# A two-layer graph convolution: 40 tiles of edges summed from h instead of 32, and denser lists of single rows

## The chip, the core and the metric

The kernel runs on one core of one Trainium2 chip. The metric is the time of one execution on the device, in microseconds (us). Five engines work beside each other, each in its own order: PE (TensorE, with its weight loads as PEld), DVE (VectorE), ACT (ScalarE), POOL (GpSimd) and SP (SyncE). SP, ACT and POOL also issue DMAs.

## The reference

There are N = 12500 nodes with 128 features and E = 200000 edges, sorted by their destination. An edge has a source, a destination and one of R = 8 types. Two layers of a relational graph convolution are followed by a residual and a layer norm:

```
W[r]     = sum_b comp[l, r, b] * basis[l, b]              # 8 matrices of 128 x 128
msg[e]   = h[src[e]] @ W[type[e]]
mean[n,r]= sum of msg over the edges (dst = n, type = r) / max(their number, 1)
h_new[n] = relu(sum_r mean[n, r] + h[n] @ root[l] + bias[l])
h        = h_new + h                                      # after layer 1 and after layer 2
out      = layernorm(x + h)                               # over the 128 features
```

## The kernel before, in words

**Tiles and octets.** The edges are cut into 1563 tiles of 128. Eight tiles are an octet (`Q = 8`); there are 196 octets in a layer, the last of 3 tiles. Each layer is one loop over the octets. A tile's 128 source rows are brought in by one indirect DMA (L814, POOL), and PE multiplies them with a 128-column or 256-column matrix that DVE makes from the destinations (L1240): it has the edge's weight, 1 over its count, where a column stands for the edge's destination, and zeros elsewhere.

**Layer 1** gathers rows of x, sums them by destination and type (L1340), multiplies by the eight W[r] (L1372) and places the result in the nodes' accumulator (L1403). When 128 nodes are done, they become a column tile of `h`, which stays in SBUF with features on the partitions (98 node tiles); and the products of these nodes with all eight W[r] of layer 2 go to a table `y_d` in HBM of 100000 rows, one for each node and type (L1558).

**Layer 2** gathers rows of that table by (source, type) and adds them straight into the nodes' accumulator (`add_rows`, L1726): two PSUM tiles in turn, 256 columns each.

**POOL's queue** holds nothing but gathers. A gather of octet q + 5 is issued at step q (`AHEAD = 5`) into one of seven buffers (`rows_r`), and it waits until PE is through with the octet that had the buffer before. The last gathers (from octet 190 on) also wait for the newest octet that PE was given before them (`after`, the cell `done`).

Two things take tiles off POOL's queue in layer 2:

*Lists of single rows* (`lists[1]`, `lone_rows`). A tile of a list isn't gathered; its 128 rows are brought in by 128 DMAs of one row each, with addresses from registers, in chunks of 32. One list is on SP's queue, one on ACT's, each with four host tiles (`sT_f`) in turn. A list takes the tiles from t0 to t1 in steps of `by`. A chunk stands in its queue's order up to 15 octets ahead of its use, one chunk an octet on ACT. SP's queue also holds the loads of x and the stores of the result, and ACT's the square roots of the norms (L1834).

*Octets summed from h* (`SUMMED`, `summed`). An entry `served: (first, end)` says that octet `served` isn't gathered from the table; its sums of source rows are made from `h` in a pass over all 98 node tiles, spread over the octets first to end. For each node tile PE turns it (L1610, `turn`), DVE copies it out of PSUM (L1618) and makes a one-hot matrix of the octet's 1024 sources (L1619, `ready`), and one octet later PE multiplies the two into two PSUM banks, 512 columns each (L1628, `sums`). In the four octets after a pass DVE and PE turn, weigh and multiply the result by W[r] (L1641 to L1674), and at octet `served` one matmul adds it to the accumulator (`place_sums`, L1698). A pass takes its node tiles evenly: `takes[first + j * n // NT]`, with n its number of octets.

**Order inside a step q of layer 2.** POOL: the gathers of q + 5. SP and ACT: chunks of the lists. DVE: copies and one-hots of the pass (`summing(q, 0)`). PE: `add_rows(q)`. DVE: the matrices of octet q + 2, which wait until PE has read octet q's, in one of two buffers. PE: the pass's matmuls and the turning of its next node tiles (`summing(q, 1)`). Then one step of a norm, if one is under way (`todo`): after eight node tiles are done, 1024 rows are turned back, added to x and normalized; the square root is a step on ACT, and DVE's reciprocal of it (L1838) comes six steps later. At every second octet a node tile is finished (L1424, L1428, L1447).

The order on every engine is thus fixed by the program; an engine waits where a semaphore tells it to, and what stands behind the waiting instruction on the same engine waits too.

Of the kernel before, what the change touches and what calls it, by code (L numbers as in the profile page):

```python
# [428 lines left out]
def ordered_path(  # L429
# [60 lines left out]
    DONE = NT - 4  # L490
    LONG = 9
    JOINED = [(1112, 84, 132), (1504, 135, 183)]
    SUMMED = {52: (3, 45), 98: (49, 91), 144: (95, 137), 190: (141, 183)}
    assert D == P and R * K == P and B == BF + 1 and 1 < TL and LAST < P and BF % 4 == 0 and Q == G and N % 2 == 0
    main = slice(HALO, HALO + P)

# [182 lines left out]
    def floats(t, n):  # L679
        return t[:, n * P:(n + 1) * P]  # L680

    sT_f = [t.rearrange("p r g k -> p (r g k)") for t in sT_r.tiles]
# [6 lines left out]
    def hot_cells(c):  # L689
# [4 lines left out]
                                     (sel.rearrange("p g k -> p (g k)"), ["sel"], [])]),  # L694
         ("ACT", 13 * Q + 2, 46 * Q, 8 * Q, 16, 10, [(floats(yr_f, j), yr_cells, yr_cells) for j in range(5)]),
         ("ACT", 53 * Q + 2, 1552, 8 * Q, 16, 10, [(floats(mixer_f, j), ["mixer"], []) for j in range(2)])],
        [("SP", 62, 1552, 49, 32, 15, [(floats(sT_f[0], j), [("sT", 0, 0), ("sT", 0, 1)], []) for j in range(4)]),
         ("ACT", 63, 1552, 49, 32, 15, [(floats(sT_f[1], j), [("sT", 1, 0), ("sT", 1, 1)], []) for j in range(4)])]]
    single, at_row = [{}, {}], [0, 0]
    for l in range(L):  # L700
        for k, (_, t0, t1, by, _, _, hosts) in enumerate(lists[l]):
# [84 lines left out]
    def gather(l, q):  # L786
        if q >= NQ or l == 1 and q in SUMMED:
            return
# [433 lines left out]
    dms, sT, ys, pl, ym = {}, {}, {}, {}, {}  # L1222
    acc, carry, vs, xs, xT, wide = {}, {}, {}, {}, {}, {}

    def onehot(l, q, g=None):

        if q >= NQ and (g is None or g < 0) or l == 1 and q in SUMMED:
            return
# [453 lines left out]

    sums_of = [(s - 1, *summed(i, s, *SUMMED[s])) for i, s in enumerate(sorted(SUMMED))]

    def summing(q, part):
        for end, *f in sums_of:
            if SUMMED[end + 1][0] - LONG <= q <= end:
                f[part](q)

    def place_sums(q, k, opens, last):  # L1690
        t, c = pl.pop(q)
        o, oc = ys.pop(q)
        a, ac = acc[k]
        root_in = opens and k >= 0
        reads = [c, oc] + ([("h", k), ("w", 1, R)] if root_in else [])

        def emit():
            ins = nc.tensor.matmul(a, o, t, start=opens, stop=last and not root_in)  # L1698
            if root_in:
                ins = nc.tensor.matmul(a[:, :rows_of(k)], w_sb[:, 1, R, :], hT[:, k * P:k * P + rows_of(k)],  # L1700
                                       start=False, stop=last)
            return ins

        pe(emit, reads, [ac])
        plan.mark("PE")

    def add_rows(q, k, opens, last, between_last=None):
        if q in SUMMED:
            place_sums(q, k, opens, last)
# [363 lines left out]
    for q in range(AHEAD):  # L2073
        gather(1, q)
    summing(min(a for a, _ in SUMMED.values()) - LONG, 0)
    for n in range(2):
# [66 lines left out]
def kernel(  # L2143
# [18 lines left out]
    flag = ctx.enter_context(tc.tile_pool(name="flag", bufs=1))  # L2162
    bad = flag.tile([1, 1], I32, name="bad")
    plan = ordered_path(tc, bad, x, src, dst, et, basis, comp, root, bias, out)
    every = [mybir.EngineType.PE, mybir.EngineType.Activation, mybir.EngineType.DVE, mybir.EngineType.Pool,
             mybir.EngineType.SP]
# [36 lines left out]
```

## Time and profile before

| what | us |
|---|---|
| median of 3 runs (lowest, highest) | 3730.01 (3728.68, 3738.03) |
| the profiled execution | 3738.43 |
| its span, first to last instruction | 3736.6 |
| POOL busy / PE busy / DVE busy | 2812.0 / 2986.0 / 2354.0 |
| layer 1's gathers, first to last | 4.5 to 1882.1 |
| layer 2's gathers, first to last | 1882.4 to 3723.9 |

A line of the costliest groups reads: line, engine, operation, out<-in by the program's names, shapes, count; then the group's busy time and the mean ns of one; then the idle time of the engine just before these instructions and what ended it. "issue" as the cause means that the engine waited for nothing that the profile shows. In a list of instructions in order of time the columns are the start, the length, the engine and line, and in brackets the idle time before and what ended it. A matmul of 32-bit floats shows as two records. Matmuls are pipelined, so a length is more than the step from one start to the next.

### The profile page before, as it was taken

The numbers are of one execution on the slowest core, as the hardware profiler recorded it, in microseconds if no ns is written. First come the engines' busy times: TensorE is split into PE (matmuls) and PEld (weight loads), VectorE is DVE, ScalarE is ACT, GpSimd is POOL, SyncE is SP. The second block draws the span as 40 slices with busy tenths as digits, with TensorE's granted clock in tenths as the row PEclk, the third lists the DMA queues.
The fourth block names the chain that finished last, engine by engine and source line by source line (L and its number), as shares of the span: only waits on it lengthen the run. The fifth ranks groups of instructions, "written<-read, shape, count | busy, mean of one in ns | idle before, by whom it ended". The sixth has DMA issues, their size and how long they took to land.

```text
span 3736.6 us, 69352 instructions
## 1 busy us (share of the span) xinstructions
PE 2986.0 (80%) x13831; PEld 2137.2 (57%) x13831; DVE 2354.0 (63%) x5786; ACT 354.5 (9%) x795; POOL 2812.0 (75%) x2977
## 2 busy tenths in 40 slices
PE   5777757778877778877778888888888888798896
PEld 3666645565655556655555555555555555555554
DVE  5556435545554445445456778787777787787885
ACT  1121212111111111111100000000000000000000
POOL 7777777777777777777777777777777777777776
PEclk7999889989999999999989999999999999999998
DMA  4122123334333333332332222222222222222222
GB/s 126 55 62 61 56 89 106 117 115 123 112 101 100 91 104 106 95 106 92 99 97 56 55 56 67 67 62 67 56 73 62 62 67 62 67 66 56 68 66 61
DMA packets 159970, 299.91 MB, mean 80 GB/s; under 512 B 67108, under 2 KB 90358, under 8 KB 159534
## 3 DMA queue, kind: packets, MB, share of 16 engines
q0 software_dynamic: 95008, 194.77, 20.4%
q10 hardware_dynamic: 34755, 68.94, 5.7%
q1 hardware_dynamic: 29771, 31.73, 3.2%
q14 instruction: 325, 2.66, 0.2%
q8 instruction: 111, 1.82, 0.2%
HBM read 236.52 MB, written 58.65 MB: 79 GB/s over the span
## 4 chain that ended last, share of the span: by engine, by line
POOL 47%; issue 17%; PE 16%; DMA 9%; ACTq 4%; ACT 3%; DVE 2%; SPq 1%; POOLq 0%; DVEq 0%
POOL rows L814 47%; DMA rows<-y_d,idy 7%; PE y L1372 4%; ACTq L750 3%; PE s L1340 3%; PE s L1726 2%; PE pt L1558 1%; ACTq L745 1%; PE ct L1531 1%; ACT sT L663 1%; SPq L750 1%; ACT y_row L663 1%; DVE dm L1240 1%; PE ct L1010 1%; PE ct L1011 1%
## 5 line engine op out<-in xcount | busy, mean ns | idle before, releaser
L814 POOL DMA_INDIRECT rows<-in_x_dram,idx x1499 | 1420.0, 947 | 459.8 <-issue 451.1
L814 POOL DMA_INDIRECT rows<-y_d,idy x1469 | 1390.0, 946 | 449.8 <-issue 440.2
L1726 PE MATMUL s<-dm,rows 128*128 128x256 f32 x2932 | 777.2, 417 | 260.7 <-DMA rows<-y_d,idy 235.8
L1240 DVE TENSOR_SCALAR dm<-cols,near,w 128x256 f32<-128x256 f16 x1531 | 709.6, 537 | 386.1 <-PE s L1726 376.4
L1726 PEld LDWEIGHTS s<-dm,rows 128*128 128x128 f32 x2932 | 592.4, 210 | 376.4 <-DMA rows<-y_d,idy 233.7
L1240 DVE TENSOR_SCALAR dm<-cols,kr,w 128x128 f32<-128x128 f16 x1563 | 525.9, 403 | 137.4 <-PE s L1340 112.5
L1372 PE MATMUL y<-w_sb,sT 128*128 128x128 f32 x3136 | 443.8, 300 | 203.9 <-ACT ys L663 150.6
L1372 PEld LDWEIGHTS y<-w_sb,sT 128*128 128x128 f32 x3136 | 406.7, 209 | 240.3 <-ACT ys L663 177.6
L1340 PEld LDWEIGHTS s<-dm,rows 128*128 128x128 f32 x2998 | 382.2, 201 | 184.0 <-issue 159.1
L1340 PE MATMUL s<-dm,rows 128*128 128x128 f32 x2998 | 401.6, 287 | 100.5 <-DMA rows<-in_x_dram,idx 90.4
L1619 DVE TENSOR_TENSOR arena<-arena,cols 128x1024 f32<-128x1024 int32 x264 | 319.9, 1212 | 0.0
L1628 PE MATMUL pt<-arena,idx 128*128 128x512 f32 x528 | 269.6, 592 | 0.0
L1628 PE MATMUL y<-arena,idx 128*128 128x512 f32 x528 | 269.6, 592 | 0.0
L1558 PE MATMUL pt<-w_sb,arena 128*128 128x512 f32 (+1 forms) x386 | 206.3, 616 | 63.0 <-DVE y_row L666 43.9
L666 DVE COPY y_row<-pt 128x512 f32<-128x512 f32 x56 | 38.7, 692 | 309.9 <-PE pt L1558 309.9
L663 ACT ACTIVATE sT<-s 128x512 f32<-128x512 f32 x391 | 213.4, 605 | 87.0 <-PE s L1340 86.7
L1516 DVE TENSOR_TENSOR arena<-arena,cols 128x512 f32<-128x512 f32 (+1 forms) x196 | 125.7, 683 | 115.0 <-PE ct L1531 112.2
L1531 PE MATMUL ct<-arena 128*128 128x512 f32 x392 | 187.1, 600 | 0.0
L663 ACT ACTIVATE y_row<-pt 128x512 f32<-128x512 f32 (+1 forms) x139 | 83.0, 597 | 1044.1 <-PE s L1340 846.8
L1628 PEld LDWEIGHTS y<-arena,idx 128*128 128x128 f32 x528 | 100.3, 190 | 126.3 <-issue 126.3
L1619 DVE TENSOR_TENSOR y_row<-arena,cols 128x1024 f32<-128x1024 int32 x128 | 155.1, 1212 | 0.0
L1834 ACT ACTIVATE st<-st,eps 128x8 f32<-128x8 f32 x12 | 3.7, 310 | 1543.8 <-DMA sT<-y_d 1302.3
(253 smaller groups left out, 2300.0 us busy)
## 6 DMA issues: line engine op xcount, KB each, us to landing
sT<-y_d SPq DMA_DIRECT2D x3968, 0.5 KB
sT<-y_d ACTq DMA_DIRECT2D x3968, 0.5 KB
y_d<-y_row ACTq DMA_DIRECT2D x96, 512.0 KB
mixer<-in_x_dram ACTq DMA_DIRECT2D x2304, 0.5 KB
rows<-in_x_dram,idx POOLq DMA_INDIRECT x1499
rows<-y_d,idy POOLq DMA_INDIRECT x1469
jmp<-in_x_dram SPq DMA_DIRECT2D x1408, 0.5 KB
comp_sb<-in_x_dram SPq DMA_DIRECT2D x1408, 0.5 KB
```

Of the source, the lines that this page charges most:

```text
L663: act(lambda: nc.scalar.activation(out_t, in_t, AF.Copy), reads, writes)
L750: return [eng.dma_start(o[j * ch + i:j * ch + i + 1, :].bitcast(byte), table_b[bass.ds(v, 4 * D)].rearrange("(p d) -> p d", p=1)) for i, v ...
L814: ins.append(nc.gpsimd.indirect_dma_start(out=t[:, i - q * Q, :], out_offset=None, in_=table_t, in_offset=bass.IndirectOffsetOnAxis(ap=ids ...
L1240: emits.append(lambda i=i: nc.vector.tensor_scalar(t[:, i - q * Q, :wide], cols[:, :wide], ids[:, i:i + 1], w[:, i:i + 1], op0=ALU.is_equa ...
L1340: last = nc.tensor.matmul(s_b[i // 4][0][:, i % 4, :], lones[i][0] if i in lones else t[:, i, :], d[:, i, :], start=True, stop=True)
L1372: last = nc.tensor.matmul(y[:m], t[:, r, :nt, :].rearrange("p t k -> p (t k)"), w_sb[:, 0, r, :], start=(r == 0), stop=(r == R - 1))
L1516: vec(lambda j=j, p=p, o=o: nc.vector.tensor_tensor(o[:p], e_t[:p], x_node[:p, j:j + 1].to_broadcast([p, M * P]), op=ALU.is_equal), [e_c, ...
L1531: pe(lambda j=j, p=p, i=i, t=t, o=o: nc.tensor.matmul(b.rearrange("p t c -> p (t c)"), t[:p, i * D:(i + 1) * D], o[:p], start=j == 0, stop ...
L1558: pe(lambda: nc.tensor.matmul(hb[:n].rearrange("p r d -> p (r d)"), hT[:, j * P:j * P + n], w_sb[:, 1, k * H:(k + 1) * H, :].rearrange("p ...
L1619: vec(lambda j=j, e=e: nc.vector.tensor_tensor(e, edge, node_p[:, j:j + 1].to_broadcast([P, Q * P]), op=ALU.is_equal), [edge_c, "node"], h ...
L1628: pe(lambda j=j, m=m, o=o, e=e, h=h, b=b: nc.tensor.matmul(b.rearrange("p t c -> p (t c)"), o[:m], e[:m, 4 * h * P:4 * h * P + 4 * P], sta ...
L1726: ins = nc.tensor.matmul(a, lones[i][0] if i in lones else t[:, i, :], d[:, i, :], start=(opens and i == 0), stop=(last and i == n - 1 and ...
```

## The change

Five octets are summed from h in layer 2 instead of four (40 tiles instead of 32). The passes have 34, 34, 34, 34 and 33 octets, where four had 43 each; the gaps of three octets between passes and the end of the last pass at octet 183 are the same. The summed octets are 44, 80, 117, 155 and 191, where they were 52, 98, 144 and 190. The two lists of single rows of layer 2 take every 47th tile instead of every 49th, from the same first tiles: 32 tiles each instead of 31, the last ones 1519 and 1520 instead of 1532 and 1533. Nothing else is edited; layer 1 does the same work.

```diff
-    SUMMED = {52: (3, 45), 98: (49, 91), 144: (95, 137), 190: (141, 183)}
+    SUMMED = {44: (3, 36), 80: (40, 73), 117: (77, 110), 155: (114, 147), 191: (151, 183)}
...
-        [("SP", 62, 1552, 49, 32, 15, [(floats(sT_f[0], j), [("sT", 0, 0), ("sT", 0, 1)], []) for j in range(4)]),
-         ("ACT", 63, 1552, 49, 32, 15, [(floats(sT_f[1], j), [("sT", 1, 0), ("sT", 1, 1)], []) for j in range(4)])]]
+        [("SP", 62, 1552, 47, 32, 15, [(floats(sT_f[0], j), [("sT", 0, 0), ("sT", 0, 1)], []) for j in range(4)]),
+         ("ACT", 63, 1552, 47, 32, 15, [(floats(sT_f[1], j), [("sT", 1, 0), ("sT", 1, 1)], []) for j in range(4)])]]
```

## The prediction

> **What bounds the kernel now.** I read the page first (busy shares, the chain, the costliest groups), then three stretches of the span, then the waits of layer 2, then engines in order of time where the change adds work.
>
> ```profile
> span 3736.6 us, 69352 instructions
> ...
> PE 2986.0 (80%) x13831; PEld 2137.2 (57%) x13831; DVE 2354.0 (63%) x5786; ACT 354.5 (9%) x795; POOL 2812.0 (75%) x2977
> ...
> POOL 47%; issue 17%; PE 16%; DMA 9%; ACTq 4%; ACT 3%; DVE 2%; SPq 1%; POOLq 0%; DVEq 0%
> ...
> L814 POOL DMA_INDIRECT rows<-in_x_dram,idx x1499 | 1420.0, 947 | 459.8 <-issue 451.1
> L814 POOL DMA_INDIRECT rows<-y_d,idy x1469 | 1390.0, 946 | 449.8 <-issue 440.2
> ```
>
> PE has the largest busy share, yet the chain is POOL's. Layer 2's 1469 gathers cost 1390.0 + 449.8 = 1839.8 us, 1.2524 us each, and of the idle part 440.2 us is "issue": POOL waiting for nothing that the profile shows. With layer 1's 1499 gathers (1879.8 us) that is 3719.6 of 3736.6 us. One gather more or less is 1.25 us of the span as long as nothing makes POOL wait.
>
> ```profile
> 400.00:600.00 200.00, 127.08 (x767) 105.04 (x768) 83.83 (x261) 33.56 (x75) 151.43 (x160) 0.86 0.27 84
> 2400.00:2600.00 200.00, 180.01 (x631) 117.12 (x630) 163.90 (x354) 0.31 (x1) 151.33 (x160) 0.97 0.28 64
> 1882.00:3724.00 1842.00, 1562.70 (x5536) 1039.03 (x5535) 1391.63 (x3001) 9.56 (x22) 1390.98 (x1471) 0.94 0.28 65
> ```
>
> ```profile
> POOL rows L814 <- issue: 431.7, 1413, 0.3
> DVE dm L1240 <- PE s L1726: 360.0, 136, 13.0
> PE s L1726 <- DMA rows<-y_d,idy: 237.6, 101, 7.4
> ```
>
> The stretches (PE, weight loads, DVE, ACT, POOL, then the clock) show POOL at the same 151 us in 200 in either layer. In layer 2 PE is busy 85% and DVE 76%, but PE's long wait is for gathered rows and DVE's is for PE: both follow POOL.
>
> **The change, part by part.** *Gathers.* A fifth octet is summed from h instead of gathered: 8 tiles less. The two lists of single rows grow from 31 to 32 tiles each: 2 less. 10 x 1.2524 = 12.5 us off POOL. That is the whole gain, if the rest stays hidden.
>
> *PE and DVE in a pass.* The fifth pass adds 98 node tiles, and a pass has 34 octets for 43, so up to 3 node tiles fall on an octet, 2.9 on the mean for 2.3.
>
> ```profile
> 2411.04 0.49 PE L1610 MATMUL ct<-ident,arena 128*128 128x128 f32 x3
> 2411.37 0.60 PE L1726 MATMUL s<-dm,rows 128*128 128x256 f32 x2
> ...
> 2412.02 3.19 PE L1726 MATMUL s<-dm,rows 128*128 128x256 f32 x14
> 2415.05 1.02 PE L1628 MATMUL pt<-y_row,idx 128*128 128x512 f32 x2
> 2415.91 1.02 PE L1628 MATMUL y<-y_row,idx 128*128 128x512 f32 x2
> ```
>
> ```profile
> 2479.28 3.71 DVE L1240 TENSOR_SCALAR dm<-cols,near,w 128x256 f32<-128x256 f16 x8 [1.56 <-PE s L1726]
> 2482.90 0.20 DVE L1838 RECIPROCAL st<-st 128x8 f32<-128x8 f32 x1
> ...
> 2483.45 0.29 DVE L1618 COPY idx<-ct 128x128 f32<-128x128 f32 x1
> 2483.65 1.22 DVE L1619 TENSOR_TENSOR arena<-arena,cols 128x1024 f32<-128x1024 int32 x1
> 2484.78 0.29 DVE L1618 COPY idx<-ct 128x128 f32<-128x128 f32 x1
> ```
>
> From start to start on PE: seven tiles take 3.03 us, so eight 3.46; half of a node tile's work 0.86, so a node tile 1.72; three transposes 0.33. An octet with three node tiles is 3.46 + 5.16 + 0.33 = 8.95 us at full clock, 9.5 at layer 2's mean clock of 0.94. On DVE eight one-hots take 3.62 and a node tile 1.33: 3.62 + 3.99 = 7.6, some 8.4 with the finish and a share of the norms. POOL's octet after the change is 8 x (1 - 64/1523) = 7.66 gathers, 9.6 us. Both stay under it, PE only just. Over the whole layer PE goes from 1562.7 to about 1562.7 + 98 x 1.72/0.94 + 98 x 0.11/0.94 - 8 x 0.43 = 1750 us, 96% of 1829.5; DVE to 1391.6 + 98 x 1.33 = 1522, 83%. The fifth summed octet's own last steps (24 small matmuls, copies) are some 5 us on PE, and SP gets one more load of an octet's indices; both lie inside the same slack. I cost this at nothing. The cover is POOL's time; if it were gone, the price would be PE's 187 us.
>
> *How far PE may be late.* There are 7 row buffers, so POOL waits for PE only when PE ends an octet later than six octets of gathers, 6 x 9.6 = 57.6 us, after that octet's last gather.
>
> ```profile
> 3603.05 11.00 DMA rows<-y_d,idy
> 3615.01 3.02 PE s L1726 x14
> ```
>
> Here a gather lands 11.0 us after its issue and PE is through 15.0 us after it. Some 42 us stay spare.
>
> *Single rows.* The lists issue 256 more one-row DMAs on SP and ACT, which also issue everything else there in order. ACT carries the norm's square root between them, and DVE's reciprocal waits for it.
>
> ```profile
> 1904.81 265.62 ACTq L750 DMA_DIRECT2D sT<-y_d  x640
> ...
> 2172.82 162.08 ACTq L750 DMA_DIRECT2D sT<-y_d  x384
> 2334.95 0.31 ACT L1834 ACTIVATE st<-st,eps 128x8 f32<-128x8 f32 x1 [162.88 <-DMA sT<-y_d]
> 2337.27 120.27 ACTq L750 DMA_DIRECT2D sT<-y_d  x288
> 2457.59 0.31 ACT L1834 ACTIVATE st<-st,eps 128x8 f32<-128x8 f32 x1 [122.33 <-DMA sT<-y_d]
> ```
>
> ```profile
> 2335.30 0.20 DVE L1838 RECIPROCAL st<-st 128x8 f32<-128x8 f32 x1 [1.49 <-ACT st L1834]
> ```
>
> ```profile
> L1838 DVE RECIPROCAL st<-st x12: 195/198/205, 2185.5 to 3719.3; 128x8 f32<-128x8 f32 x12
> ```
>
> ACT issues without a pause: (2457.59 - 1904.81) / 41 chunks of 32 = 13.5 us a chunk, 54 us a tile. With 195 octets in 1842 us an octet is 9.45 us, so a list needed a tile every 49/8 x 9.45 = 58 us; now every 47/8 x 9.38 = 55 us. ACT still keeps up, but hardly catches up. It starts late (the second root already holds DVE up by 1.49 us), and now stays so. In the changed order of instructions 44 chunks stand ahead of the third root, 41 before: it comes 3 x 13.5 = 40 us later, at 2498, while DVE wants it at 2482.9. So DVE will wait some 15 us there. By the same count for the others (20, 32, 41, 52, 63, 72, 84, 94, 104, 115 chunks become 21, 32, 44, 54, 65, 76, 87, 98, 108, 120), set against the twelve reciprocals' starts less the gathers saved by then, I estimate that seven of the first ten norms wait, 5 to 20 us each, some 70 us in all. DVE is in order: behind its reciprocal stand the copies and one-hots that PE needs. But a single wait of 20 us is less than the 42 spare, norms are some 150 us apart, and PE wins back up to 9.6 - 8.95 = 0.65 us an octet in a pass and about 5 in each of four octets without node tiles, some 40 us per pass. So: nothing, bounded by 0 and 28 us (70 less the 42 spare).
>
> *Tail.* Passes still end at octet 183; the last summed octet is 191, not 190.
>
> ```profile
> 3688.10 0.95 POOL L814 DMA_INDIRECT rows<-y_d,idy  x1 [0.30 <-issue]
> 3690.39 0.95 POOL L814 DMA_INDIRECT rows<-y_d,idy  x1 [1.33 <-PE s L1726]
> ...
> 3722.93 0.95 POOL L814 DMA_INDIRECT rows<-y_d,idy  x1 [0.30 <-issue]
> ```
>
> Octet 192's gathers wait for PE's octet 189, 1.03 us beyond the usual 0.30. With octet 190 gathered between them, 7 gathers rather than 6, that wait may go: 0 to 1 us, I take 0.5. The 12.7 us after the last gather stay.
>
> *Sum.* The profiled execution took 3738.43 us, 3736.6 of span and 1.8 around it. 12.5 + 0.5 = 13.0 off gives 3725.4. The median of the runs shown, 3730.0, is 8.4 under the profiled one, so against it 3717.0, 0.35% less.
>
> *A rule that speaks against it.* The row: POOL's gather takes 947 ns in layer 1 and 946 in layer 2, though DVE's share doubles between the two stretches (83.83 to 163.90 us of 200). The Trainium skill (SBUF — State Buffer, "SBUF: two separate sides") says that VectorE and GpSimd share a port pair that is locked for a whole instruction, so that DMAs issued from GpSimd starve while VectorE runs certain operations. By that rule the added 130 us of DVE would hold POOL for up to that long; by the row it holds it for nothing.
>
> **The rivals.** *The late root reaches POOL (slower).* Place: DVE's reciprocal behind ACT's roots. If PE wins back nothing of what it loses, 70 us less 42 spare = 28 us of POOL waits, 3717 + 28 = 3745. It decides once PE ends an octet over 57.6 us behind its last gather. For it: the second root above comes late even now. Against: the slack per pass.
>
> *PE becomes the pass's bound.* At the clock of the poorest stretch, 0.86, the octet is 8.95/0.86 = 10.4 us, 0.8 x 34 = 27 us lost per pass against 20 to 25 regained between passes; after five passes the spare is used up or nearly so: 0 to 15 us, 3725. For it: PE at 96%. Against: the clock is 0.97 where PE is busiest. The Trainium skill (TensorE: Matmul & The Clock Gate, Part 1) says the clock is halved after idle windows, and the two stretches agree.
>
> *Single rows late at the end.* ACT's last tile is issued 128 x 0.42 = 54 us later and needed 13 us earlier. If ACT slows by a few per cent, PE waits where nothing follows that could hide it: 5 to 15 us, about 3727.
>
> *DVE's lock on POOL.* If POOL is held for a quarter to all of the 130 us, 3750 to 3847.
>
> **How the numbers follow.** The forecast has 0.68. Of that 0.06 falls within 0.3% (11.2 us, about what a measurement of this kernel can tell from no change), because 13.0 is so near it and the runs shown spread over 9 us. The late root has 0.13, PE's bound 0.08 (half of it within 0.3%), late single rows 0.07 (within), the lock 0.02, anything else slower 0.02. So faster 0.62, same 0.06 + 0.04 + 0.07 = 0.17, slower 0.13 + 0.04 + 0.02 + 0.02 = 0.21. The forecast's own range is 3711 to 3721 (12.5 to 13.5 off, with some 4 us of scatter on the median). The range of 8 in 10 reaches on over PE's bound and the late rows, to 3733; the late root and the lock stay outside.
>
> **What would show it.** Layer 2 with 1459 gathers, still 1.25 us each with "issue" as releaser, POOL's wait for PE under some 10 us: the gain is right. PE's wait for rows far below 237.6 us and PE's busy share in a pass above 90%: the ledger is right. Reciprocals of the norms that wait for ACT, 5 to 20 us each: the late root is right, and harmless if POOL does not wait. Wrong if POOL's gathers wait for PE in the middle of passes, if the gather's mean leaves 946 ns, or if over 13 us pass between the last gather and the end.

## The result, and the profile after

The changed kernel takes 3740.79 us (median of 9 runs, 3735.93 to 3742.77), the kernel before 3730.61 beside it: a ratio of 1.0026, with a 95% interval from 1.0018 to 1.0035. So it is 0.26% slower, where 0.35% less was forecast (3717.0 us, range of 8 in 10 from 3711 to 3733). The gathers became fewer as said; the time came back in two waits at the end.

From the page of the changed kernel: span, busy shares, the chain, and the group of layer 2's gathers.

```profile
span 3740.5 us, 71111 instructions
...
PE 3086.4 (83%) x14347; PEld 2170.8 (58%) x14347; DVE 2485.0 (66%) x5990; ACT 354.5 (9%) x795; POOL 2801.9 (75%) x2967
...
POOL 30%; PE 25%; issue 15%; ACTq 12%; SPq 10%; DMA 4%; DVE 3%; ACT 2%; POOLq 0%; DVEq 0%
...
L814 POOL DMA_INDIRECT rows<-y_d,idy x1459 | 1380.1, 946 | 465.2 <-issue 437.2
```

There are 10 gathers fewer, of the same 946 ns. But of 465.2 us of idle time 28.0 are no longer "issue" (before: 9.6), and the chain has moved: POOL from 47% to 30%, SP's and ACT's queues from 5% to 22%. POOL's instructions in order of time show where it waits (start, length, and in brackets the idle time before and what ended it):

```profile
3675.40 0.94 POOL L814 DMA_INDIRECT rows<-y_d,idy  x1 [9.01 <-PE s L1726]
...
3682.90 0.94 POOL L814 DMA_INDIRECT rows<-y_d,idy  x1 [0.30 <-issue]
3694.94 0.94 POOL L814 DMA_INDIRECT rows<-y_d,idy  x1 [11.10 <-PE s L1726]
```

These are the first gathers of octets 190 and 192. The gathers from octet 190 on are issued two octets ahead of PE, not five (`CLOSE = 2`), and wait for PE's newest octet, 187 and 189 here. Before, the only such wait was 1.33 us. The account of the two traces closes to 0.4 us: 12.5 us of gathers less, 19.5 us of waits more there (20.1 less twice the usual 0.30), 1.0 us for the old wait and some 1.1 us at the layer's opening less, together +4.9; the last gather ends at 3728.4 us, where it was 3723.9.

The two traced executions are only 3.9 us apart (3738.43 and 3742.31), the medians 10.2. The rest is probably the pace of the gathers, which is not the same in every execution: from the start of one to the start of the next pass 1251 to 1252 ns in both of these traces, in layer 1 too, but 1249 ns in four traces of the experiments on chips where the kernel before takes 3730 to 3737 us. Over 2960 gathers that is an estimated 7 us, and the traced execution of the kernel before lies 7.8 us above the median. No execution of the kernel before at the faster pace was traced, so this stays open; by it the change costs some 4 us at the same pace, and ratios that lie less than 0.002 apart don't rank two kernels by themselves. The waits in the traces do.

Why PE is late, in three views of the changed kernel. First the waits of layer 2 (total, times, longest):

```profile
PE s L1726 <- DMA rows<-y_d,idy: 58.8, 30, 7.7
DVE arena L1619 <- DMA arena<-in_src_dram: 51.1, 2, 33.9
DVE st L1838 <- ACT st L1834: 47.3, 5, 20.1
```

PE's wait for gathered rows fell from 237.6 us: it follows POOL no longer. DVE waits twice for the indices of a summed octet, loaded by SP, and for roots of ACT. Next SP's DMAs in order of time, each row a group issued one behind the other:

```profile
3329.79 17.54 SPq L750 DMA_DIRECT2D sT<-y_d  x44
3347.39 0.48 SPq L660 DMA_DIRECT2D arena<-in_src_dram  x1
...
3515.25 0.38 SPq L660 DMA_DIRECT2D out_dram<-x_g  x1
3531.09 0.36 SPq L660 DMA_DIRECT2D x_g<-in_x_dram  x1
3533.76 151.67 SPq L750 DMA_DIRECT2D sT<-y_d  x384
```

The indices that DVE waits for until 3364.4 leave SP only at 3347.4, behind chunks of the list. Between the store of a result and the load of x into its buffer SP stands 15.8 us until the store has landed. And the list's last three tiles (384 rows) take SP until 3685.4. Then PE:

```profile
3687.96 1.19 PE L1726 MATMUL s<-dm,rows 128*128 128x256 f32 x2 [4.62 <-DMA sT<-y_d]
```

PE begins octet 189, whose tile 1519 is SP's last, 2.5 us after its last row is issued, and waited for it. In the kernel before, SP was through with its last tile 60 us before PE's start on it (3639.87, and 3699.8 for octet 191):

```profile
3589.74 50.13 SPq L750 DMA_DIRECT2D sT<-y_d  x128
```

SP's list lasted from 1902.9 to 3685.4, 1782.5 us or 55.7 a tile. At POOL's pace one is needed every 1459 x 1.2524 / 195 x 47/8 = 55.0 us. In the kernel before it took 56.0 us a tile (1904.6 to 3639.9, 31 tiles), and one was needed every 1469 x 1.2524 / 195 x 49/8 = 57.8 us: there SP won 1.8 us with each tile, here it loses 0.7.

### The profile page after: what moved, and what is told of

It is laid out like the page before. It is cut to its first block, busy times and chain, and to the rows that moved or that the text cites. A ratio compares the mean times of both kernels' runs of the same rounds, so it can differ in the third digit from the quotient of the medians.

```text
span 3740.5 us, 71111 instructions
## 1 busy us (share of the span) xinstructions
PE 3086.4 (83%) x14347; PEld 2170.8 (58%) x14347; DVE 2485.0 (66%) x5990; ACT 354.5 (9%) x795; POOL 2801.9 (75%) x2967
## 4 chain that ended last, share of the span: by engine, by line
POOL 30%; PE 25%; issue 15%; ACTq 12%; SPq 10%; DMA 4%; DVE 3%; ACT 2%; POOLq 0%; DVEq 0%
POOL rows L814 30%; ACTq L750 9%; SPq L750 8%; PE s L1726 6%; PE y L1628 4%; PE pt L1628 4%; ACTq L745 2%; PE y L1372 2%; PE s L1340 2%; SPq L745 2%; DMA rows<-y_d,idy 1%; ACT sT L663 1%; DMA rows<-in_x_dram,idx 1%; DVE dm L1240 1%; PE ct L1010 1%
## 5 line engine op out<-in xcount | busy, mean ns | idle before, releaser
L814 POOL DMA_INDIRECT rows<-y_d,idy x1459 | 1380.1, 946 | 465.2 <-issue 437.2
L1726 PE MATMUL s<-dm,rows 128*128 128x256 f32 x2912 | 713.9, 394 | 79.6 <-DMA rows<-y_d,idy 58.8
L1726 PEld LDWEIGHTS s<-dm,rows 128*128 128x128 f32 x2912 | 555.6, 198 | 164.8 <-DMA rows<-y_d,idy 48.3
L1340 PEld LDWEIGHTS s<-dm,rows 128*128 128x128 f32 x2998 | 376.9, 199 | 195.1 <-issue 173.9
L1619 DVE TENSOR_TENSOR arena<-arena,cols 128x1024 f32<-128x1024 int32 x330 | 398.6, 1208 | 51.1 <-DMA arena<-in_src_dram 51.1
L1628 PE MATMUL pt<-arena,idx 128*128 128x512 f32 x660 | 337.0, 592 | 0.0
L1628 PE MATMUL y<-arena,idx 128*128 128x512 f32 x660 | 337.0, 592 | 0.0
L1628 PEld LDWEIGHTS y<-arena,idx 128*128 128x128 f32 x660 | 125.4, 190 | 157.9 <-issue 157.9
L1618 DVE COPY idx<-ct 128x128 f32<-128x128 f32 x490 | 138.5, 283 | 99.3 <-PE ct L1610 93.3
L1619 DVE TENSOR_TENSOR y_row<-arena,cols 128x1024 f32<-128x1024 int32 x160 | 193.2, 1208 | 0.0
L1628 PEld LDWEIGHTS pt<-arena,idx 128*128 128x128 f32 x660 | 125.3, 190 | 99.3 <-issue 92.3
```

Of the source, the lines that this page charges most:

```text
L814: ins.append(nc.gpsimd.indirect_dma_start(out=t[:, i - q * Q, :], out_offset=None, in_=table_t, in_offset=bass.IndirectOffsetOnAxis(ap=ids ...
L1340: last = nc.tensor.matmul(s_b[i // 4][0][:, i % 4, :], lones[i][0] if i in lones else t[:, i, :], d[:, i, :], start=True, stop=True)
L1619: vec(lambda j=j, e=e: nc.vector.tensor_tensor(e, edge, node_p[:, j:j + 1].to_broadcast([P, Q * P]), op=ALU.is_equal), [edge_c, "node"], h ...
L1628: pe(lambda j=j, m=m, o=o, e=e, h=h, b=b: nc.tensor.matmul(b.rearrange("p t c -> p (t c)"), o[:m], e[:m, 4 * h * P:4 * h * P + 4 * P], sta ...
L1726: ins = nc.tensor.matmul(a, lones[i][0] if i in lones else t[:, i, :], d[:, i, :], start=(opens and i == 0), stop=(last and i == n - 1 and ...
```

## The experiments

All ratios are to the kernel before on the same chip, with 95% intervals. After the trace three theories stood against each other: the passes are too full for PE; late indices or late roots, which DVE waits for, make PE late; or SP's queue as a whole is too slow for a list that takes every 47th tile. The expectations name them by letters in the first four runs (theory A: the lists make the queues late, and late indices and the last tile do the harm; the rivals stand beside it) and by numbers from then on (theory 1: SP's queue; theory 2: ACT's roots; theory 3: the roots and indices that stand behind chunks).

**Each half alone.** Two kernels: the five passes with lists by 49, and the old four passes with lists by 47.

```diff
-        [("SP", 62, 1552, 47, ...   ("ACT", 63, 1552, 47, ...
+        [("SP", 72, 1552, 49, ...   ("ACT", 73, 1552, 49, ...
```

> The five passes of the changed kernel with lists of every 49th tile, as before (first tiles 72 and 73, since a list may not touch a summed octet): 8 gathers fewer than before, 62 single-row tiles as before; all work is kept. Theory A: SP and ACT keep their old margin, 58 us of use against 54 of issuing for a tile, so indices and roots come in time, PE is late by under 15 us and POOL does not wait at the end; 8 x 1.25 = 10 us faster than before, 3719 to 3723 us. Rival C (passes too full for PE): as slow as the changed kernel, 3735 to 3742.

```diff
-    SUMMED = {44: (3, 36), 80: (40, 73), 117: (77, 110), 155: (114, 147), 191: (151, 183)}
+    SUMMED = {52: (3, 45), 98: (49, 91), 144: (95, 137), 190: (141, 183)}
...
-        [("SP", 62, 1552, 47, ...   ("ACT", 63, 1552, 47, ...
+        [("SP", 61, 1552, 47, ...   ("ACT", 62, 1552, 47, ...
```

> The kernel before with lists of every 47th tile (first tiles 61 and 62, since a list may not touch a summed octet): 2 gathers fewer; all work is kept. Theory A: SP and ACT fall behind as in the changed kernel, indices and roots come late, but PE has slack in passes of 43 octets and wins it back; only a last single-row tile can still cost, so 3726 to 3733 us. Rival E (the lists alone cost what the change costs): 3738 to 3745.

The passes alone: 0.9971 [0.9960, 0.9983], 10.7 us of the median (3726.14 for 3736.85), as 8 gathers of 1.25 would have it. The lists alone: 1.0023 [1.0013, 1.0033], though they save 2 gathers; theory A, which had PE win this back in the longer passes, was wrong here. In POOL's instructions the first wait for PE in the last octets is 0.55 us with the passes and this with the lists:

```profile
3692.29 0.95 POOL L814 DMA_INDIRECT rows<-y_d,idy  x1 [15.79 <-PE s L1726]
```

So the denser passes are not too much for PE and DVE, and the loss comes with the lists.

**The late indices, and the last tile.** The loads of indices placed 20 octets ahead of a pass, not 9; and SP's list without its last tile, which is gathered.

```diff
-    LONG = 9
+    LONG = 20
```

> The changed kernel with the load of a pass's 1024 indices put 20 octets ahead of the pass instead of 9 (one constant); all its work is kept. Theory A (SP's queue runs some 100 us behind its place in the program because of the single rows, so that the fourth and fifth pass's indices come late and hold DVE up by 33.9 and 17.2 us, and PE never wins that back before the last gathers, which wait for PE): both waits for the indices vanish, the 9.0 us wait of POOL near 3675 us goes, the later one of 11.1 us stays at least in part because the last single-row tile is issued as late as before; 3727 to 3733 us. Rival B (ACT's late square roots, 47 us of waits on DVE, are what PE never wins back): 3737 to 3742. Rival C (a pass simply holds more work for PE than POOL's time for an octet): 3738 to 3742, PE as late as before at octet 187.

```diff
-        [("SP", 62, 1552, 47, ...
+        [("SP", 62, 1515, 47, ...
```

> The changed kernel with the last tile of SP's list (1519, in octet 189) gathered by POOL instead, one gather more; all work is kept. Theory A: only the second of POOL's two waits at the end is touched; it shrinks from 11.1 to 4 to 6 us, because PE is late at octet 189 by itself, the first one of 9.0 stays; 3734 to 3738 us. Rival D (the last single-row tile, issued until 3685 us, is the whole cost at the end): both waits shrink, 3724 to 3730. If that tile costs nothing: 3741 to 3743, one gather more.

With early indices DVE's 51.1 us are gone, and the time stays: 1.0016 [1.0007, 1.0026]. POOL waits 19.37 and 4.70 us, DVE 69.5 us for roots, PE 27.2 us for single rows. So the late indices alone are not the cause, as theory A had it; other waits took their place. Without tile 1519 POOL still waits 9.42 and 3.44 us, 1.0001 [0.9991, 1.0010]: 6 us of the loss by the waits (7.3 us less waiting, 1.25 us for the gather more) or 9 by the ratio were the last tile's, no more.

**The stall by itself.** Layer 2's last gathers don't wait for PE's newest octet.

```diff
-        after = [("done", l)] if q >= NQ - LATE else []
+        after = [("done", l)] if q >= NQ - LATE and l == 0 else []
```

> The changed kernel, but layer 2's gathers from octet 190 on don't wait for the newest octet that PE was given; they still wait for their buffers. It prices the 19.5 us that POOL waits there for PE. If PE's lateness costs time only through that wait: POOL's wait falls to under 2 us, PE catches up in the last octets, which have no node tiles, and the time falls by 12 to 19 us, to 0.9975 to 0.9990. If PE is itself what ends last: the last gather ends earlier, but more than 20 us pass behind it, and the time stays at 1.001 to 1.003.

1.0006 [0.9996, 1.0015], between the two expectations. The last gather ends at 3706.1 us, 22 earlier, but now 24.5 us pass behind it while PE catches up. Of the 20 us of stall some 12 (24.5 less 12.1 behind the last gather of the changed kernel) are lateness of PE that the end pays in any case.

**Which of the two queues.** One list by 49, the other left at 47.

```diff
-        [("SP", 62, 1552, 47, ...
+        [("SP", 73, 1552, 49, ...
```

> The changed kernel, but SP's list takes every 49th tile from 73 on (31 tiles); ACT's keeps every 47th from 63 (32 tiles). One gather more than the changed kernel. Theory 1, SP's list of DMAs is the bound of layer 2 at every 47th tile: SP has 50 us and more to spare at each tile, PE's lag stays under 20 us, POOL waits under 2 us for PE at the end, and the time is that of the passes alone less one gather of 1.25 us: 0.9967 of the kernel before. Theory 2, ACT's late roots cost the time (DVE's reciprocal waits): they are still there, 45 us in four or more, and so is the loss: 1.001 to 1.003.

```diff
-         ("ACT", 63, 1552, 47, ...
+         ("ACT", 72, 1552, 49, ...
```

> The mirror of the run with SP's list by 49: the changed kernel, but ACT's list takes every 49th tile from 72 on (31 tiles); SP's keeps every 47th from 62. Theory 1 (SP's list is the bound): as slow as the changed kernel, 1.002 to 1.003, SP's slack under 16 us from the middle on, and POOL waits 15 to 20 us for PE at the end, although DVE's waits for ACT's roots fall under 10 us in all. Theory 2 (ACT's roots): the waits are gone and with them the loss, 0.997.

SP eased: 0.9974 [0.9965, 0.9983]. SP's last tile is issued by 3638.8, and POOL has no wait over 0.42 us at the end, though DVE still waits for roots as in the changed kernel:

```profile
DVE st L1838 <- ACT st L1834: 42.8, 7, 16.7
```

So 43 us of late roots are hidden as long as SP is in time. This kernel and the one without tile 1519 have the same numbers of tiles on SP (31), on ACT (32) and of gathers; they differ only in how closely SP's tiles follow one another and so where they stand, and the closer ones cost POOL 12.9 us of waits and 0.0027 of the time. That points to the rate of SP's list, not to its length. ACT eased: 0.9986 [0.9977, 0.9995], which theory 1 had wrong. The indices still come late and SP has no margin at the end, but it ends its list 11.9 us earlier than in the changed kernel, and POOL doesn't wait for PE there (first its wait for indices, then SP's last three tiles):

```profile
DVE arena L1619 <- DMA arena<-in_src_dram: 41.2, 2, 35.3
```

```profile
3521.76 151.76 SPq L750 DMA_DIRECT2D sT<-y_d  x384
```

The list's end at 3673.5 is thus just early enough, that at 3685.4 is 12 us late, and the second wait of the changed kernel is 11.10. The earlier end has two sources. Inside a chunk SP's mean step from the start of one single-row DMA to the next is 345.1 ns here and 347.3 in the changed kernel; 2.2 ns x 3968 steps are 8.7 us. The pauses between chunks are another 3.9 us shorter (400.3 us for 404.2), and the list began 0.9 us later. The step is no sure effect of ACT's list: with both lists by 49 it is 342.4 ns with the passes alone and 345.0 in the kernel before. Nor does 0.9986 say that this remedy is worth less than the other: the gathers have the slower pace in this trace (1252 ns) and the faster with SP eased (1249), and 3.7 of the 4.7 us between the two medians show already at the end of layer 1 (1882.4 us for 1878.7), where both do the same work.

**Freeing SP of its waits.** The rows of x for norm n + 1 are loaded in the middle of norm n, long after the store that had the buffer.

```diff
-        todo.extend([turn, add, stats, aggr, root_of] + [lambda: None] * 5 + [one_by, scale, store])
+        ahead = (lambda: load_x(n + 1)) if 1 <= n <= NX - 3 else lambda: None
+        todo.extend([turn, add, stats, aggr, root_of] + [lambda: None] * 2 + [ahead] + [lambda: None] * 2 + [one_by, scale, store])
...
-                    if n + 2 < NX:
+                    if n + 2 == NX - 1:
```

> The changed kernel with both lists as it has them, but SP's loads of x for the norms are put one norm later in the order (the rows of norm n + 1 are loaded in the middle of norm n, not right behind the store of norm n - 1), so that SP doesn't wait for a store to land before it issues them. It takes some 71 us of SP's waits in 6 places away, 2.2 us per tile of its list (55.7 down to some 53.5, needed 55). Theory 1: SP's slack grows again to 25 us and more, PE's lag at octet 188 is under 10 us, POOL's wait at the end is under 5 us, and the time is 0.9965 to 0.998. If SP's issue itself (52.4 us a tile) is too slow, little changes: 1.001 to 1.003. Theory 2 (ACT's roots): no change, 1.002 to 1.003.

1.0074 [1.0061, 1.0088], the opposite of what theory 1 expected. SP is free indeed: it ends its list at 3661.6, 24 us earlier, and PE never waits for its rows. But now ACT is late. Here are a row of this kernel's waits, ACT's instructions in order of time (three tiles, 384 rows, and a root behind them) and POOL's wait:

```profile
DVE st L1838 <- ACT st L1834: 120.2, 8, 26.7
```

```profile
3406.26 167.33 ACTq L750 DMA_DIRECT2D sT<-y_d  x384
3573.64 0.31 ACT L1834 ACTIVATE st<-st,eps 128x8 f32<-128x8 f32 x1 [169.47 <-DMA sT<-y_d]
```

```profile
3697.02 0.95 POOL L814 DMA_INDIRECT rows<-y_d,idy  x1 [26.66 <-PE s L1726]
```

and of ACT in the changed kernel:

```profile
2338.72 161.60 ACTq L750 DMA_DIRECT2D sT<-y_d  x384
```

ACT now takes 167.33 / 3 = 55.8 us a tile, for 53.9 there, and needs to take no more than 55.0; over the whole list it is 55.6 for 54.7. Its mean step inside a chunk rose from 355.3 to 362.6 ns, SP's from 347.3 to 355.4. It looks as if each queue issues more slowly the less the other pauses. 120 us of late roots are not hidden where 43 were.

**Roots and indices earlier in both queues.** Chunks stand at most 10 octets ahead of their use, so that some 4 chunks fewer stand before a root or a load of indices.

```diff
-        [("SP", 62, 1552, 47, 32, 15, ...   ("ACT", 63, 1552, 47, 32, 15, ...
+        [("SP", 62, 1552, 47, 32, 10, ...   ("ACT", 63, 1552, 47, 32, 10, ...
```

> The changed kernel, but the chunks of both lists stand at most 10 octets ahead of their use, not 15. On a chip where the kernel before takes some 3730 us: theory 3 (DVE's 98 us of waits for roots and indices that stand behind chunks): DVE's waits for roots fall from 47 to under 10 us, those for indices from 51 to under 10, PE's lag at octet 188 is under 10 us, POOL's wait at the end under 3 us, 0.9965 to 0.9975. Theory 1 (SP's rows come late for PE): PE waits for them instead, over 40 us in all, POOL still waits 10 us and more, 1.000 to 1.003.

1.0063 [1.0050, 1.0077]. Among DVE's waits in the layer stands no root (up to 0.4 us at the end) and no index, but POOL waits 14.67 and 22.71 us. In place of DVE it is PE that waits:

```profile
PE s L1726 <- DMA sT<-y_d: 66.2, 9, 17.3
```

with the last of these waits, and SP's rows ahead of it:

```profile
3631.09 0.38 SPq L660 DMA_DIRECT2D out_dram<-x_g  x1
3646.90 0.36 SPq L660 DMA_DIRECT2D x_g<-in_x_dram  x1
3649.59 48.97 SPq L750 DMA_DIRECT2D sT<-y_d  x128
```

```profile
3699.64 1.19 PE L1726 MATMUL s<-dm,rows 128*128 128x256 f32 x2 [17.31 <-DMA sT<-y_d]
```

Theory 3, by which what stands behind the chunks is the price, falls. With roots and indices first, the chunks come later by as much, one wait for a store (15.8 us) falls right before the last tile, and SP ends at 3698.6. The queue is full: another order only chose who waits, and here POOL waited longer for it (37.4 us for 20.1).

**On other chips.** There are chips on which the kernel before takes 5621 to 5630 us, and some of the runs fell on them. There SP's mean step inside a chunk is 610 to 624 ns, for 347, and in layer 2 the list of 32 tiles lasts from 2804 to 5559 us, 86 us a tile (second run with both lists 10 octets ahead). The chain of that run:

```profile
SPq 55%; issue 33%; another core or an unknown queue 4%; PE 4%; DVE 2%; ACTq 1%; DMA 1%; ACT 1%; POOL 0%; DVEq 0%
```

PE waits 692 us for single rows there, 32 times, and POOL 757 us for PE. POOL is no bound, so these runs don't settle what happens at POOL's end, and the times that their expectations give, which were for the other kind of chip, decide nothing.

> The changed kernel, but the chunks of both lists stand at most 10 octets ahead of their use in their queues, not 15; same tiles, same passes. In ACT's order 28, 40, 51, 61, 72 chunks stand ahead of the roots where the changed kernel has 32, 44, 54, 65, 76: about 4 chunks of 13.6 us, 54 us earlier; in SP's order 76 and 100 chunks stand ahead of the loads of indices that came late, for 80 and 104. Theory 3, the two queues are each nearly full (54 to 56 us of issue for a tile needed every 55 us), and what the layer loses are the 98 us in which DVE waits for the roots and the indices that stand behind chunks: DVE's waits for roots fall from 47 to under 10 us, those for indices from 51 to under 10, PE's lag at octet 188 is under 10 us, POOL's wait at the end under 3 us, 0.9965 to 0.9975. Theory 1 (the rows of SP's list themselves are late for PE): they stay late, PE waits for them instead (over 40 us in all), POOL still waits 10 us and more, 1.000 to 1.003.

0.9975 [0.9956, 0.9994], and again:

> The changed kernel, but the chunks of both lists stand at most 10 octets ahead of their use, not 15; run again, since the first time a single-row DMA took half as long again on the whole chip. Theory 3 (DVE's 98 us of waits for roots and indices that stand behind chunks): DVE's waits for roots fall from 47 to under 10 us, those for indices from 51 to under 10, PE's lag at octet 188 is under 10 us, POOL's wait at the end under 3 us, 0.9965 to 0.9975. Theory 1 (SP's rows are late for PE): PE waits for them instead, over 40 us in all, POOL still waits 10 us and more, 1.000 to 1.003.

0.9990 [0.9971, 1.0010]. ACT's list alone 10 octets ahead:

> As the run with both lists 10 octets ahead, but ACT's alone; SP's stays at 15. Theory 3: DVE's waits for roots go (47 to under 10 us), those for indices stay at about 50, a sum like that of the run with ACT by 49 (41 us), and so like its time: 0.998 to 0.999, with POOL's wait at the end under 5 us. If the roots are harmless and the indices alone cost: 1.001 to 1.003.

0.9975 [0.9952, 0.9998], and again 0.9994 [0.9973, 1.0015]:

> ACT's list alone 10 octets ahead, SP's at 15, run again. Theory 3: DVE's waits for roots go (47 to under 10 us), those for indices stay at about 50, a sum like that of the run with ACT by 49 (41 us), and so its time: 0.998 to 0.999, POOL's wait at the end under 5 us. If the late indices alone cost as much as both: 1.001 to 1.003.

The later loads of x with both lists 10 octets ahead:

> The kernel with SP's loads of x one norm later (which came out at 1.0074, with 120 us of DVE's waits for roots), and both lists 10 octets ahead instead of 15. Theory 3: the roots no longer stand behind late chunks, the 120 us fall to under 20 us, and with them the whole loss: 0.9965 to 0.9985. If the slower issue of ACT (361.8 ns from one single-row DMA to the next, for 354.6) is what costs, through rows that land late for PE: PE's waits for single rows grow by as much as DVE's fall, 1.003 to 1.008.

0.9982 [0.9958, 1.0006], and twice again 0.9984 [0.9967, 1.0001] and 0.9990 [0.9968, 1.0012]:

> SP's loads of x one norm later and both lists 10 octets ahead, run again. Theory 3: the 120 us of waits for roots fall to under 20 us, and the whole loss of the run with the later loads alone (1.0074) with them: 0.9965 to 0.9985. If ACT's slower issue costs through rows that come late for PE, PE's waits for single rows take the roots' place: 1.003 to 1.008.

> The changed kernel with SP's loads of x one norm later, and both lists 10 octets ahead. On a chip where the kernel before takes some 3730 us. Theory 1 (SP's queue is the bound, and with the later loads alone the roots on ACT took its place): SP's slack stays at 40 us and more, the 120 us of waits for roots fall to under 20 us, PE's lag at octet 188 under 15 us, POOL's stall under 8 us, 0.9965 to 0.999. If ACT's own issue is too slow at every 47th tile (55.8 us a tile in the run with the later loads, needed 55): the rows of ACT's list come late for PE in the roots' place, its last tile is issued after 3685 and POOL still waits 15 us and more, 1.002 to 1.007.

Both lists 10 octets ahead and the last gathers free:

> Both lists 10 octets ahead, and layer 2's last gathers don't wait for PE's newest octet. If the lists' place in the queues already takes POOL's stall away, this is the same as without it, within 0.0007: 0.9965 to 0.9975. If 10 us of stall are left there, it is 0.0025 faster than without.

1.0003 [0.9987, 1.0020]. All of these hold the same 32 tiles on SP, and no two differ by more than their intervals. The one kernel with a tile fewer on SP's list differs (SP by 49, ACT by 47 and 10 octets ahead):

> The kernel with SP's list by 49 and ACT's by 47 (0.9974), with ACT's chunks 10 octets ahead instead of 15. Its 42 us of waits for roots go. Theory 1: they were hidden, so the time stays within 0.0007 of 0.9974. If DVE's waits cost time even where POOL doesn't stall: 0.9960 to 0.9967.

0.9915 [0.9883, 0.9946], neither of the two that were expected, and 50 us less than the kernel with the later loads beside it (5564.17 for 5614.48), where one tile takes 87 to 88 us of SP's list. The two also differ in the place of SP's last tile, 1543 in octet 192 here and 1519 in octet 189 there: in their traces 32 us and 60 us follow it. Why this kernel beats the kernel before, which has 31 tiles on SP too, stays open (the kernel before was not traced on such a chip), and so does whether freeing both queues at once would keep the gain on a chip of the first kind.

## Why the prediction was wrong, point by point

- *Gathers, 12.5 us.* Right: 1459 gathers at 946 ns, and 8 of the 10 give 10.7 us where nothing else is late.
- *PE and DVE in a pass, nothing.* Right: with the passes alone POOL waits 0.55 us, and DVE waits for no root (up to 0.4 us) and no index. Of the two sizes behind it DVE's was right (1523 us busy in layer 2, forecast 1522); PE's busy time rose by 104 us (1564.0 to 1668.0 between 1882 and 3728 us), not 187, while its mean granted clock rose from 0.94 to 0.96.
- *Single rows on ACT.* The mechanism is right, the size two thirds: 47.3 us in five waits, for some 70 in seven; the third root came at 2500.4, forecast 2498. Costed at nothing, and hidden indeed where it was alone (43 us, 0.9974).
- *SP, "one more load of an octet's indices; both lie inside the same slack".* This step failed. ACT's chunks were counted, SP's never, though its list grew in the same way and its queue holds more: 55.7 us a tile with the waits for stores, for 55.0 needed. The slack of 60 us that the list had at its end was used up, indices came 17 to 34 us late and the last tile 11 us too late.
- *How far PE may be late, 57.6 us and 42 spare.* Right in the middle of the layer: PE ended octets up to 56.2 us behind their last gather, and POOL didn't wait. With the later loads of x PE passed the limit (60.2 us at octet 174), and POOL waited 2.94 us, which is 60.2 - 57.6 and the usual 0.30; the same happened with the last gathers free (60.5 us at octet 119; 1.64 and 1.96). Wrong at the end, and this is the second step that failed: there the gathers wait for PE's newest octet, named in the tail's step but not in this one. Between the last gather of octet 187 and the first of octet 190 stand 15 gathers, so the spare is 15 x 1.25 = 18.8 us, not 57.6 (20.0 with SP by 49, where octet 189 has no single-row tile). PE ended octet 187 14.8 us behind its last gather with SP by 49 and 14.3 with ACT by 49, and POOL waited for nothing; it was 27.5 us in the changed kernel, and POOL waited 27.5 - 18.8 + 0.3 = 9.0.
- *Tail, 0.5 us gained.* 20.1 us of waits instead, for 1.33.
- *Sum, 8.4 us from the traced execution to the median.* The sum took it that the changed kernel would run at the pace of the untraced executions of the kernel before. Its traced execution, near its median, has the slower pace; some 6 of the 24 us between 3717.0 and 3740.79 are probably this and no work of the change.
- *Rivals.* "Single rows late at the end" had the place, the end of a list, but named ACT's; SP's cost 11.10 us (priced 5 to 15), and PE's lag another 9.01. "The late root reaches POOL" gave 3745 us, near the result, but by a cause that by itself stays hidden; it is real only with SP freed, at 120 us. PE as the pass's bound is out. So is the lock: DVE's busy time rose from 2354.0 to 2485.0 us and the gather's mean stayed at 946 ns. The Trainium skill (SBUF — State Buffer, "SBUF: two separate sides") has DMAs issued from GpSimd starve while VectorE runs certain operations; by these numbers none of the added operations does so here.

The cause as far as shown: the two lists together, at every 47th tile each, leave SP and ACT no room for what else stands in their queues, PE falls behind, and at the end the spare is 18.8 us. Both together lose the gain; with either one eased POOL has no wait at the end, and the time is 0.14 to 0.26% below that of the kernel before. How PE's lag divides among late indices, roots and rows in the changed kernel itself isn't settled, since each remedy in the queues' order moved the wait to another of the three.

Faster than both kernels are the five passes with lists by 49 (0.9971) or with SP's by 49 and ACT's by 47 (0.9974), which the intervals don't tell apart.

## What to carry to other kernels

When a change puts more work on a queue that issues DMAs, write that queue's own ledger (time per item, all its waits, against the time between two needs), for every queue that it touches. A queue without a margin can't be helped by reordering it: early roots make late rows. And the spare time of a stage is that of its tightest wait, which at the end of a kernel may be another than in the middle.

## What the hardware showed that was not expected

Two queues that issue at once seem to slow one another: SP's mean step between single-row DMAs inside a chunk was 342 to 345 ns with both lists by 49, 345 with one of them by 47, 347 to 349 with both, and 355 when its waits for stores were taken out; ACT's was 351 to 354, 353 to 354, 355 to 356 and 363. The Trainium skill (DMA: Bandwidth & Descriptors, "Issuing engines are not separate DMA queues") says that DMAs of several engines run on the same 16 DMA engines, and that starting them from several engines saves only the time of initiating them; here that time, too, was not quite saved, by 3 to 4% at most.

The same program took half as long again on some chips (5620 us), with single-row DMAs at 610 to 624 ns a step on SP and POOL no longer the bound: a margin on one chip is not one on another. The median step is 322 ns on both kinds of chip; on the slower ones some 720 to 760 of SP's 3844 or 3968 steps take over 1 us (the longest 3.5 us), on the others none does.

A gather's pace differs between executions: 1249 or 1251 to 1252 ns from one start to the next, in both layers alike, 7 us over this kernel.
